# A mixture-of-experts stage that sends each token only to its two chosen experts

## The chip, the cores and the metric

The kernel runs on one core of one Trainium2 chip. The metric is the device time of one execution, in microseconds (us). The trace comes from one profiled execution on the same kind of core; its engines are TensorE (PE, with the loading of weights shown apart as PEld), VectorE (DVE), ScalarE (ACT), GpSimd (POOL) and SyncE (SP), which only issues transfers here.

## What is computed

Two layers over 2048 tokens (4 batches of 512) of width 128. Each layer adds `s * silu(ffn)` to `x`, where `s` comes from an attention and `ffn` from a mixture of experts on the normalised `x`. The change is in the second layer's mixture:

```python
def _L1_ffn_ref(x, wg1, bg1, wg2, w_in, w_out):
    # E, H, K, G = 8, 256, 2, 32
    xt = x.reshape(-1, d)
    g = gelu(xt @ wg1 + bg1)
    probs = softmax(g @ wg2)
    top_vals, top_idx = top_k(probs, K)
    gates = zeros_like(probs).at[arange(n)[:, None], top_idx].set(top_vals)
    h = gelu(einsum('nd,edh->enh', xt, w_in))
    o = einsum('enh,ehd->end', h, w_out)
    y = einsum('ne,end->nd', gates, o)
```

Only two of the eight rows of `gates` are not zero for a token. The result of this mixture is used late, as the gate of the second layer's output: `x + s * silu(y)`.

## The kernel before

The work falls into four stages on one time line. First comes the first layer's mixture (`norm_ffn0`, 0 to 78 us in the trace) with the loading of the weights. Then the first layer's attention (`attn0`, 78 to 400 us) goes through 32 segments of 64 positions. Then the second layer's mixture (`ffn1`, 392 to 534 us). Last is the second layer's attention (`attn1`, 534 us to the end), 16 steps for each of the 4 batches.

Nearly every instruction is pinned: `pin`, `mm1`, `act1`, `vec1`, `pool1` and `dma1` (L314 to L330) record an operation and keep it in program order on its engine. So each engine works through a list written by hand, and an instruction that waits holds up all that stands behind it on its engine. The DMA queue of SP is such a list too, and so are the transfers that POOL issues. The lists are made by dictionaries of the form "after step n, also call these functions" (`between` in `attn0` and `ffn1`), and in `attn1` by the number t of the step.

In one segment n of `attn0`, TensorE makes the scores of the next segment, then `memory(n)` (L709, tiles `mm`), `update(n)` (L726, tiles `mu`), `attend(n)` (L753, tiles `dot`) and `attended(n-1)` (L776, transposes `pa`). POOL multiplies by gates and adds: L724 in `memory`, L740 in `update` (a part of the memory `mz`, which TensorE reads in `memory(n+1)`), L772 and L773 in `attend`, whose result the transposes `pa` read. The router of the second layer's first two batches is already run inside `attn0` (`sums`, `scale`, `normed`, `turned`, `hidden`, `logits`, `chosen` at segments 18 to 24).

The second layer's mixture before is dense: `ffn1` (L979) goes over 4 batches and 8 experts, 32 units in all. A unit is `up(b, e)` (L946: two matmuls 128x512 in fp32, which the trace shows as four, into tile `ph`; then one gelu on ACT) and, one unit later, `down(b, e)` (L956: eight matmuls 128x128 into tile `eo`, 16 in the trace; then four DVE operations L969 or L971 that weight the result with `gw` and add it to `acc`). Between units stand the end of `attn0` (`left[0]`, `left[1]`), the router of batches 2 and 3, and the preparation of the second attention for batch 0 (`prepare1`), whose tiles are `ptk`, `ptv`, `ptq`, `pjk`, `pjq` and `pl`, and whose DRAM pieces `kd`, `qd`, `qe` are written by SP. `opening1` (L1552) at the last unit makes the first scores of the second attention from operands that SP loads (`k<-kd`, `q<-qd`).

In a step i of `attn1` (b = i // 16, t = i % 16), TensorE makes the scores of step i+1 (`s`), then three groups of products with the values (`acc`); ACT makes `exp` and squares; DVE multiplies the two (L1548, tiles `e`), and the third group of the next step's products needs that. Side work is spread over t. At t = 11, `gate1` (L994) turns the mixture's result into the gate. POOL prepares the features of the next batch and the products L1324 and L1325 of rows that SP has loaded.

At the end a flag says whether the fast path's bounds held; if not, `run_any` computes all again on a general path.

Of the kernel before, what the change touches and what calls it, by code (L numbers as in the profile page):

```python
# [11 lines left out]

# [28 lines left out]
HF, G1 = 256, 32  # L41

# [52 lines left out]
class Kernel:  # L95
# [124 lines left out]
    def load_second(self, pool):  # L220
# [3 lines left out]
        for w in ("q", "k", "v"):  # L224
            own = pool.tile([P, D], F32, name=f"l1w{w}")
            nc.sync.dma_start(out=own, in_=i[f"L1_attn_W{w}"])

            flat = pool.tile([P, D], F32, name=f"l1b{w}f")
            nc.gpsimd.dma_start(out=flat, in_=i[f"L1_attn_b{w}"].partition_broadcast(P))
            self.wt[w] = pool.tile([P, D], F32, name=f"l1w{w}t")  # L230
            self.bt[w] = pool.tile([P, D], F32, name=f"l1b{w}t")
            for to, src in ((self.wt[w], own), (self.bt[w], flat)):
                nc.gpsimd.tensor_copy(
                    to.rearrange("p (m r d) -> p m r d", m=4, r=4),
                    src.rearrange("p (r m d) -> p m r d", m=4, r=4),
                )
            if w != "v":
                self.b1[w] = pool.tile([P, 1], F32, name=f"l1b{w}")
                own = i[f"L1_attn_b{w}"].rearrange("(r m d o) -> m r d o", m=4, r=4, o=1)
                for m in range(4):  # L240
                    nc.gpsimd.dma_start(out=self.b1[w][m * 32 : m * 32 + 32], in_=own[m])
# [63 lines left out]
    def normed(self, pool, mv, rstd, layer, n):  # L305
        xn = pool.tile([P, D], F32, name=f"xn{layer}_{n}", tag="xn", bufs=4)
        self.vec1(self.nc.vector.tensor_scalar(
            xn, self.x[:, n, :], mv[:, n, 0:1], rstd[:, n : n + 1], ALU.subtract, ALU.mult
        ))
        return xn  # L310
# [561 lines left out]

    def begin_ffn1(self, pool, psum, layer):
# [7 lines left out]
        gw = pool.tile([P, NT, NE], F32, name=f"gw{layer}")  # L881
        xnT, acc, xn, hid, out = {}, {}, {}, {}, {}
# [44 lines left out]
        def chosen(b):  # L927
# [11 lines left out]
            at = pool.tile([P, 4, 2, NE], F32, name=name("at", b), tag="at", bufs=2)  # L939
            self.vec1(v.tensor_tensor(  # L940
                at, bc(bc(self.iota, 1, 2), 1, 4), bc(idf, 3, NE), ALU.is_equal
            ))
            self.vec1(v.tensor_mul(at, at, bc(top[:, tiles(b), 0:2], 3, NE)))
            self.vec1(v.tensor_add(gw[:, tiles(b), :], at[:, :, 0], at[:, :, 1]))

# [10 lines left out]
        def down(b, e):  # L956
# [19 lines left out]
            sums, scale, normed, turned, hidden, logits, chosen, up, down  # L976
        )}, xnT=xnT, acc=acc)

    def ffn1(self, first, between, begun=False):  # L979


        late = None
        for b in range(B):
            for e in range(NE):
                if not (begun and late is None):
                    first.up(b, e)
                for f, *args in between.get((b, e), []):
                    f(*args)
                if late:
                    first.down(*late)  # L990
                late = b, e
        first.down(*late)
# [63 lines left out]
    def mixing1(self, pool, keep, psum):  # L1056
# [6 lines left out]
        self.load_second(keep)  # L1063
# [84 lines left out]
    def begin1(self):  # L1148

        nc, keep = self.nc, self.keep1  # L1150
        self.bounds = keep.tile([P, 2 * B * H1 + 2], F32, name="bounds")

        self.feat = keep.tile([P, 16, ROWS1 + P], F32, name="feat")
        nc.gpsimd.memset(self.feat[:, :, ROWS1 - 1 : ROWS1], 1.0)
        self.sets1 = []
        for k in range(2):
            strip = keep.tile([P, 4, H1, STRIP], F32, name=f"strip{k}")
            nc.gpsimd.memset(strip, 0.0)
            nc.gpsimd.memset(strip[:, :, :, 26:27], 1.0)
            lin = keep.tile([P, 2, 4, 4, 32], F32, name=f"lin{k}")  # L1160
            nc.gpsimd.memset(lin, 0.0)
            self.sets1.append((strip, lin))

        self.rows1 = keep.tile([P, 4, S], F32, name="rows1")
        self.rows2 = keep.tile([P, 4, S], F32, name="rows2")
        self.now1, self.banks1, self.inv1, self.prod1 = {}, {}, {}, {}

# [255 lines left out]
    def large1(self, flag):  # L1423
# [3 lines left out]
        every = pool.tile([P, nb + 2], F32, name="every")  # L1427

        def first():
# [3 lines left out]
            ))  # L1433
            self.pool1(nc.gpsimd.partition_all_reduce(every, bounds, P, bass_isa.ReduceOp.max))

        def second():
# [5 lines left out]
            bad = pool.tile([P, 3], F32, name="bad")  # L1442
            for k, (value, limit) in enumerate((
                (most, (LIMIT / SCALE1) ** 2), (every[:, nb : nb + 1], SUM_MAX),
                (every[:, nb + 1 : nb + 2], -SUM_MIN),
# [113 lines left out]
    def attn1(self, xnT, g1):  # L1559
# [4 lines left out]
        with tc.tile_pool(name="a1", bufs=2) as self.a1, tc.tile_pool(  # L1564
# [59 lines left out]
            for i in range(n):  # L1624
                b, t = i // 16, i % 16
                if t == 11:
# [32 lines left out]
                if b == B - 1 and t in (3, 11):  # L1659
                    large[t // 8]()  # L1660
                late = [f for f in [rest(x) for rest, x in ready] if f]
# [302 lines left out]
    def run(self):  # L1964
# [15 lines left out]
        with tc.tile_pool(name="wf1", bufs=1) as wf1, tc.tile_pool(name="f1", bufs=1) as f1:  # L1980
            stack = ExitStack()
            w0 = stack.enter_context(tc.tile_pool(name="w0", bufs=1))
            with tc.tile_pool(name="wf0", bufs=1) as wf0:
                self.load_first(wf0, w0)
                xnT, g0 = self.norm_ffn0(0, lambda pool, psum: self.mixing1(pool, late, psum))
                self.load_memory(w0)
            self.load_experts(wf1)
            with tc.tile_pool(name="ap", bufs=1, space=PSUM) as psum:
# [8 lines left out]
                    24: [(first.chosen, 1)], 30.5: [(first.up, 0, 0)],  # L1997
                })
                second, prep = ExitStack(), []

                def begin():
                    stack.close()
                    keep, a1q, dram = (
                        tc.tile_pool(name="a1k", bufs=1, side="right"),
                        tc.tile_pool(name="a1q", bufs=1, side="right"),
                        tc.tile_pool(name="a1d", bufs=2, space=bass.MemoryType.DRAM),
                    )
                    self.keep1, self.a1q, self.a1d = map(second.enter_context, (keep, a1q, dram))
                    self.begin1()
                    prep.extend(self.prepare1(0, first.xnT, psum, ("t", 2)).values())  # L2010

                def prepare():
                    pe, rest, *evict = prep.pop(0)
                    ps = pe()
                    rest(evict[0](ps) if evict else ps)

                between = {
                    (0, 1): [(left[0],)], (0, 2): [(left[1],), (begin,)], (0, 3): [(first.sums, 2)],
                    (0, 4): [(first.sums, 3)], (0, 5): [(first.scale, 2, 4), (first.normed, 2)],
                    (0, 6): [(first.turned, 2), (first.normed, 3)],  # L2020
                    (0, 7): [(first.turned, 3), (first.hidden, 2)],
                    (1, 0): [(first.hidden, 3)], (1, 1): [(first.logits, 2), (first.logits, 3)],
                    (1, 2): [(first.chosen, 2)], (1, 4): [(first.chosen, 3)],
                }
                for k in range(11):
                    between[1 + (5 + k) // NE, (5 + k) % NE] = [(prepare,)]
                between[B - 1, NE - 1] = [(self.opening1, psum, "w", 3)]
                self.ffn1(first, between, True)
# [6 lines left out]
    def run_any(self):  # L2035

        tc = self.tc
        with tc.tile_pool(name="wf1c", bufs=1) as wf1:
# [6 lines left out]
            with tc.tile_pool(name="f1c", bufs=1) as pool, tc.tile_pool(  # L2045
# [6 lines left out]
                for b in range(B):  # L2052
                    for f in ("normed", "turned", "hidden", "logits", "chosen"):
                        getattr(first, f)(b)
                self.ffn1(first, {})
# [40 lines left out]
```

## Time and profile before

| | us |
|---|---|
| median of 3 timed runs (lowest, highest) | 888.13 (888.01, 890.93) |
| the profiled execution | 890.56 |
| its span in the trace | 888.8 |
| stage of the second layer's mixture, 400 to 534 us: PE busy of 134.0 | 131.7 |
| the same stage: DVE, ACT, POOL busy | 53.2, 44.8, 24.6 |
| second attention, 534 to 585 us: PE, DVE, ACT, POOL busy of 51.0 | 48.4, 38.9, 43.0, 40.9 |
| second attention, 622 us to the end: PE, DVE, ACT, POOL busy of 267 | 248.3, 193.9, 183.7, 108.9 |

A row of the timeline has the start in us, the length in us, the engine, the line of the kernel, the operation, `output<-input`, the shapes, and how many such instructions were merged. In brackets stands how long the engine was idle just before, and whose end it waited for. A group row ends with busy time, mean length of one in ns, and the idle time before.

### The profile page before, as it was taken

To read this page: it belongs to the slowest core of one execution; us is meant where nothing else is said; L and a number is where in the kernel's file an instruction comes from. 1 tells how busy PE (TensorE), PEld (TensorE's weight loads), DVE (VectorE), ACT (ScalarE), POOL (GpSimd) and SP (SyncE) were. 2 spreads that over 40 slices of the span, in tenths; PEclk is the share of its full clock that TensorE was granted. 3 is DMA by queue.
4 is the path that set the end of the run, shared out by engine and by line. 5 is a ranking of instruction groups with operands and counts; after the bars stand their busy time and mean duration, and the time that the engine had idled before them with its cause. 6 is when DMAs were issued, how large, how long until landed. Compare 5 with 4: busy or idle time off the path is not lost. (4 is left out here: it accounts for less than half of the span.)

```text
span 888.8 us, 19127 instructions
## 1 busy us (share of the span) xinstructions
PE 850.0 (96%) x7660; PEld 525.9 (59%) x7660; DVE 596.3 (67%) x1202; ACT 520.1 (59%) x692; POOL 383.4 (43%) x471
## 2 busy tenths in 40 slices
PE   8998899999999999989999998999999999989996
PEld 4565688898888969877677772333234224322324
DVE  7774666667668868863353337687876888677684
ACT  3433565656566665642432249778776787768780
POOL 7840244545444433563033007853934492441112
PEclk9999999999999989999999999999999999999999
DMA  8501421212122121100005002354151324130000
GB/s 213 140 14 39 117 62 43 80 25 84 37 61 72 38 60 37 27 1 1 1 1 178 1 1 72 126 164 110 53 172 53 87 92 128 58 87 30 1 13 15
DMA packets 77055, 57.64 MB, mean 65 GB/s; under 512 B 40176, under 2 KB 65040, under 8 KB 76960
## 3 DMA queue, kind: packets, MB, share of 16 engines
q1 hardware_dynamic: 74768, 54.94, 21.1%
q0 software_dynamic: 1616, 1.16, 0.8%
q8 instruction: 62, 1.02, 0.5%
q10 hardware_dynamic: 576, 0.26, 0.1%
q14 instruction: 33, 0.27, 0.1%
HBM read 35.36 MB, written 20.97 MB: 63 GB/s over the span
## 5 line engine op out<-in xcount | busy, mean ns | idle before, releaser
L1548 DVE TENSOR_TENSOR e<-e,e 128x1024 f32<-128x1024 f32 x126 | 182.2, 1486 | 78.1 <-ACT e L321 78.1
L318 PE MATMUL acc<-e,strip 128*32 128x512 f32 x1520 | 185.0, 601 | 11.8 <-DVE bank L1590 10.4
L321 ACT ACTIVATE e<-s 128x1024 f32<-128x1024 f32 x126 | 122.1, 1022 | 69.0 <-PE s L318 69.0
L321 ACT ACTIVATE e<-e 128x1024 f32<-128x1024 f32 x126 | 126.4, 1060 | 0.0
L318 PEld LDWEIGHTS acc<-e,strip 128*32 128x32 f32 x1520 | 44.9, 110 | 125.5 <-issue 86.6
L321 ACT ACTIVATE h<-ph 128x1024 f32<-128x1024 f32 x32 | 32.8, 1024 | 87.5 <-PE ph L318 87.4
L318 PEld LDWEIGHTS eo<-w_out,h 128*128 128x128 f32 x512 | 62.5, 196 | 11.7 <-issue 10.4
L321 ACT ACTIVATE pj<-pp 128x512 f32<-128x512 f32 x64 | 38.2, 597 | 50.4 <-PE pp L318 50.2
L318 PE MATMUL eo<-w_out,h 128*128 128x128 f32 x512 | 64.5, 281 | 1.0 <-DVE g L971 0.8
L772 POOL TENSOR_TENSOR t<-t,gate 128x512 f32<-128x512 f32 x32 | 40.8, 1276 | 56.9 <-DVE t L705 41.7
L971 DVE SCALAR_TENSOR_TENSOR g<-eo,gw,g 128x128 f32<-128x128 f32 x112 | 31.5, 344 | 48.7 <-PE eo L318 48.7
L318 PE MATMUL dot<-vone,E 128*128 128x65 f32 x512 | 61.1, 273 | 0.0
L318 PEld LDWEIGHTS dot<-vone,E 128*128 128x128 f32 x512 | 59.8, 192 | 1.1 <-issue 0.8
L318 PE MATMUL ph<-xnT,w_in 128*128 128x512 f32 x128 | 60.3, 594 | 0.0
L724 POOL TENSOR_TENSOR t<-t,gate 128x512 f32<-128x512 f32 x32 | 40.9, 1279 | 33.7 <-DVE t L705 33.7
L747 DVE TENSOR_TENSOR mz<-mz,mu 64x512 f32<-64x512 f32 x56 | 38.4, 685 | 19.3 <-PE mu L318 18.7
L667 DVE SCALAR_TENSOR_TENSOR elu<-elu,up 128x512 f32<-128x512 f32 x60 | 42.4, 707 | 7.2 <-ACT up L321 6.4
L773 POOL TENSOR_TENSOR t<-t,t 128x512 f32<-128x512 f32 x32 | 45.7, 1429 | 2.5
L321 ACT ACTIVATE attT<-pa 128x512 f32<-128x512 f32 x32 | 19.1, 597 | 46.2 <-PE pa L783 46.2
L643 DVE TENSOR_TENSOR E<-sc,cap 128x1024 f32<-128x1024 f32 x32 | 39.0, 1220 | 9.6 <-PE sc L318 7.0
L740 POOL TENSOR_TENSOR mz<-mz,zs 64x8 f32<-64x8 f32 x56 | 11.7, 209 | 70.3 <-DVE zs L672 61.6
L321 ACT ACTIVATE E<-E 128x1024 f32<-128x1024 f32 x32 | 33.6, 1051 | 11.5 <-DVE E L643 11.5
(279 smaller groups left out, 1629.4 us busy)
## 6 DMA issues: line engine op xcount, KB each, us to landing
vd<-vt SPq DMA_DIRECT2D x32, 256.0 KB
vone<-vd SPq DMA_DIRECT2D x64, 128.0 KB
k<-kd SPq DMA_DIRECT2D x16, 256.0 KB
q<-qd SPq DMA_DIRECT2D x16, 256.0 KB
rows<-qd SPq DMA_DIRECT2D x64, 64.0 KB
other<-qe SPq DMA_DIRECT2D x16, 256.0 KB
kd<-partk SPq DMA_DIRECT2D x12, 256.0 KB
qd<-partq SPq DMA_DIRECT2D x12, 256.0 KB
```

The lines of the kernel that those rows point to most:

```text
L318: return self.pin(self.nc.tensor.matmul(*args, **kw))
L321: return self.pin(self.nc.scalar.activation(*args, **kw))
L643: self.vec1(nc.vector.tensor_tensor(e.rearrange("p x hp c -> p (x hp) c"), ps.rearrange("p x hp c -> p (x hp) c"), bc(self.cap.rearrange(" ...
L667: self.vec1(nc.vector.scalar_tensor_tensor(t, t, 1.0, up, ALU.min, ALU.add))
L724: nc.gpsimd.tensor_mul(t, t, self.gate)
L740: nc.gpsimd.tensor_add(new[half, :, :, p, DK].rearrange("d hp a -> d (hp a)"), old[half, :, :, p, DK].rearrange("d hp a -> d (hp a)"), seg ...
L747: self.vec1(nc.vector.tensor_tensor(new[half, :, :, p, 0:DK], old[half, :, :, p, 0:DK], ps[half, :, :, p * 64 : p * 64 + 64].rearrange("d ...
L772: nc.gpsimd.tensor_mul(t, t, gate2)
L773: nc.gpsimd.tensor_add(t, t, seg[n]["t1"])
L971: self.vec1(v.scalar_tensor_tensor(acc[b][:, k, :], eo[:, k, :], w, acc[b][:, k, :], ALU.mult, ALU.add))
L1548: self.vec1(self.nc.vector.tensor_mul(t, src[0][pair], src[1][pair]))
```

## The change

The second layer's mixture no longer runs every expert on every token. The tokens are taken in two halves of two batches (1024 tokens, 2048 choices each). For each half, 8 experts have 512 places each in a DRAM tensor (`rows_in`), which is filled with zeros at the start of the program. The choice of a token gets a place: its rank among the choices of that expert so far, from matmuls with a triangular and an all-ones matrix (`placed`). POOL then writes each token's normalised row to its two places by indirect DMAs (`sent`: 8 for a batch, 128 rows of 512 bytes each). A unit is now one expert of one half: SP fetches 512 rows (`fetched`), TensorE turns them (`faced`), `up1`, `gelu1` and `down1` follow, and SP writes the result to `rows_out`. That makes 16 units in place of 32. In `attn1` POOL gathers, for each batch, the two result rows of each token by 8 indirect DMAs at t = 8 (`back1`), and DVE weights and adds them at t = 10 (`together`); the gate follows at t = 12 in place of 11. If an expert of a half gets more than 512 tokens, the flag sends the program to the general path, which keeps the dense form.

With that, things move. The place and the sending of batches 0 and 1 stand at segments 24 to 26 of `attn0`; the fetches of the first two units at segment 29; the end of `attn0` now comes before unit 1 without expert work between; the router of batches 2 and 3 stands at units 0 to 4; and `prepare1` runs in another order, from unit 0 on. Half of the clearing of the second attention's tiles (`zeros1(1)`) moves to step 0 of `attn1`.

```diff
+    def begin_rows(self, pool, dram):
+        spill = (NE + 1) * ROOM
+        self.rows_in = [dram.tile([spill + 16 * P, D], F32, name=f"in{h}") for h in range(2)]
+        self.rows_out = [dram.tile([NE * ROOM, D], F32, name=f"out{h}") for h in range(2)]
+        zero = pool.tile([P, S], F32, name="zero")
+        nc.gpsimd.memset(zero, 0.0)
+        for t in self.rows_in:
+            nc.sync.dma_start(
+                out=t[0 : NE * ROOM].rearrange("(p n r) d -> p n (r d)", p=P, r=4),
+                in_=bc(zero, 1, NE),
+            )
...
+        def placed(b):
+            (at, e), own = hid[b], mask[:, tiles(b)]
+            self.vec1(v.tensor_copy(self.share[:, tiles(b)], top[:, tiles(b), 0:2]))
+            self.vec1(v.tensor_add(own, at[:, :, 0], at[:, :, 1]))
+            ps = narrow("rank", b)[:, :, 0:NE]
+            parts = [(ps, self.lower, own)]
+            parts += [(ps[:, k + 1 :], self.ones, bc(own[:, k], 1, 3 - k)) for k in range(3)]
+            if b % 2:
+                parts += [(ps, self.ones, bc(mask[:, b * 4 - 4 + k], 1, 4)) for k in range(4)]
+            for k, (out_, lhsT, rhs) in enumerate(parts):
+                self.mm1(
+                    out_, lhsT=lhsT, rhs=rhs, start=(k == 0), stop=(k == len(parts) - 1)
+                )
+            self.vec1(v.tensor_tensor(at, at, bc(ps, 2, 2), ALU.mult))
...
+        def sent(b):
+            for k in range(4):
+                for c in range(2):
+                    self.pool1(nc.gpsimd.indirect_dma_start(
+                        out=self.places[b // 2][b % 2 * 8 + k * 2 + c],
+                        out_offset=bass.IndirectOffsetOnAxis(
+                            ap=self.slots[:, b * 4 + k, c : c + 1], axis=0
+                        ),
+                        in_=xn[b][k], in_offset=None,
+                    ))
...
+        def faced(i):
+            pt = narrow("xgt", i)
+            for k in range(4):
+                self.pin(nc.tensor.transpose(pt[:, k, :], out["in", i][:, k], self.ident))
+            out["t", i] = pool.tile([P, 4, P], F32, name=name("xt", i), tag="xt", bufs=2)
+            self.act1(out["t", i], pt, AF.Copy)
...
+    def ffn1(self, first, between):
+        n = 2 * NE
+        for i in range(n):
+            if i:
+                first.up1(i)
+            first.gelu1(i)
+            for f, *args in between.get(i, []):
+                f(*args)
+            if i + 1 < n:
+                first.faced(i + 1)
+            for k in [i + 3] if i + 3 < NE else [NE, NE + 1] if i == NE - 2 else [i + 3] * (
+                NE - 2 < i < n - 3
+            ):
+                first.fetched(k)
+            if i:
+                first.down1(i - 1)
+        first.down1(n - 1)
+
+    def back1(self, b):
+        nc, acc = self.nc, self.of_batch("g", 1, b)
+        other = self.a1.tile([P, 4, D], F32, name=f"bk{b}", tag="pr1", bufs=2)
+        for c, t in enumerate((acc, other)):
+            for k in range(4):
+                self.pool1(nc.gpsimd.indirect_dma_start(
+                    out=t[:, k, :], out_offset=None, in_=self.rows_out[b // 2][:],
+                    in_offset=bass.IndirectOffsetOnAxis(
+                        ap=self.found[:, b * 4 + k, c : c + 1], axis=0
+                    ),
+                ))
...
+                if i == 0:
+                    self.zeros1(1)
+                if t == 8:
+                    g1[b], together = self.back1(b)
+                if t == 12:
                     self.gate1(pool, g1[b], b)
...
+                if t == 10:
+                    together()
...
-                    24: [(first.chosen, 1)], 30.5: [(first.up, 0, 0)],
+                    24: [(first.chosen, 1), (first.placed, 0)],
+                    25: [(first.placed, 1), (first.sent, 0)], 26: [(first.sent, 1)],
+                    29: [(first.fetched, 0), (first.fetched, 1)], 30.5: [(first.faced, 0)],
                 })
+                left[0]()
+                first.up1(0)
+                first.fetched(2)
+                left[1]()
...
+                        0: [(prepare, 2), (first.sums, 2), (first.sums, 3), (first.scale, 2, 4)],
+                        1: [(prepare, 3), (first.normed, 2), (first.turned, 2)],
+                        2: [(first.normed, 3), (first.turned, 3), (first.hidden, 2)],
+                        3: [(first.hidden, 3), (first.logits, 2), (first.logits, 3),
+                            (first.chosen, 2), (first.chosen, 3)],
+                        4: [(first.placed, 2), (first.sent, 2), (first.placed, 3),
+                            (first.sent, 3)],
+                        5: [(prepare, 0)], 7: [(prepare, 1), (prepare, 9)],
+                        10: [(prepare, 4)], 11: [(prepare, 5)], 12: [(prepare, 6), (prepare, 7)],
+                        13: [(prepare, 8)], 14: [(prepare, 10)],
+                        15: [(self.opening1, psum, "w", 3)],
```

`up1`, `gelu1` and `down1` have the matmuls of `up` and `down`, and `down1` ends with one DVE copy of the whole tile `eo` and a transfer to `rows_out`.

## Prediction

> **What bounds the kernel now.** I read the page's timeline first, then the group rows, then TensorE's order of time in the stage that the change rewrites.
>
> ```profile
> span 888.8 us, 19127 instructions
> ...
> PE   8998899999999999989999998999999999989996
> ...
> POOL 7840244545444433563033007853934492441112
> ...
> L318 PE MATMUL eo<-w_out,h 128*128 128x128 f32 x512 | 64.5, 281 | 1.0 <-DVE g L971 0.8
> ...
> L318 PE MATMUL ph<-xnT,w_in 128*128 128x512 f32 x128 | 60.3, 594 | 0.0
> ```
>
> TensorE is busy nearly everywhere, and `ph` and `eo` of the second mixture waited for next to nothing. So that stage is TensorE's. A unit's cadence, from TensorE's order of time:
>
> ```profile
> 411.17 1.88 PE L318 MATMUL ph<-xnT,w_in 128*128 128x512 f32 x4
> 412.89 1.95 PE L318 MATMUL eo<-w_out,h 128*128 128x128 f32 x16
> 414.68 1.88 PE L318 MATMUL ph<-xnT,w_in 128*128 128x512 f32 x4
> ```
>
> From start to start `ph` takes 1.72 us and `eo` 1.79, so 3.51 for a unit, 112 for all 32. The change halves that. What it adds is mostly on POOL, and waits.
>
> **The unknown price, c.** The trace has no indirect DMA. Let c be the time for which one holds POOL; there are 32 writes and 32 gathers. Nearest rows of POOL's order of time, and landing from the table of issues:
>
> ```profile
> 3.06 0.54 POOL L116 DMA_DIRECT2D sg<-in_L_ffn_Sg_dram  x1
> ...
> 810.02 1.50 POOL L1434 PARTITION_ALL_REDUCE every<-bounds  x1 [7.13 <-DVE bounds L1431]
> ```
> ```profile
> sg<-in_L_ffn_Sg_dram POOLq DMA_DIRECT2D x1, 64.0 KB, 2.9
> ```
>
> `sg` moves the same 128 rows of 512 bytes without indices: 0.54, the lower end; indices can't make it cheaper. The only instruction in which POOL works across partitions takes 1.50, the upper end. I take 0.75: the direct issue plus 0.21, POOL's mean for its smallest two-input operation (`mz<-mz,zs`, 64x8), for reading the 128 indices. It is nearest to the direct row because the work differs by the indices only. Landing: 2.5 us after issue (rows of 64 KB: 2.5 to 3.5). [...]
>
> **Part by part** (c = 0.75 in brackets).
>
> *Start.* POOL gets five small operations ahead of `pick0b`, about 1.3 us, against 2.3 us between the end of `pick0b` (13.84) and the first `pw` (16.18). SP gets 4 MB of zeros behind the first weights; DVE's first use of a late load is at 47.95, with inputs ready at 42. 0 to 3, I take 0.5.
>
> *Router places in `attn0`.* `rank` of batch 0 stands behind `pa` at 341.0. It needs DVE's mask, which is queued behind `chosen` of batch 1:
>
> ```profile
> 345.31 0.23 DVE L940 TENSOR_TENSOR at<-iota,idf 128x64 f32<-128x64 f32 x1
> ```
>
> With two small operations that is 345.9: TensorE, without idle time from 341 to 362, waits 5.0, and the matmuls are 0.4. Batch 1's `rank` waits from 353.3 to 354.8 for the mask behind DVE's `t`, plus 0.6. Together +7.5.
>
> *Sending from `attn0`.* The first eight writes stand behind POOL's 357.5, ahead of these:
>
> ```profile
> 357.88 1.28 POOL L724 TENSOR_TENSOR t<-t,gate 128x512 f32<-128x512 f32 x1 [0.36 <-DVE t L705]
> 361.26 0.49 POOL L740 TENSOR_TENSOR mz<-mz,zs 64x8 f32<-64x8 f32 x2 [2.09 <-DVE zs L672]
> ```
> ```profile
> 363.17 1.11 PE L318 MATMUL mm<-mz,elu 128*64 128x130 f32 x16
> ```
>
> `mm` reads `mz`. With the writes `mz` ends at 357.5 + 8c + 1.77, so `mm` loses 8c − 3.9. After L772 and L773 (2.9) come the next eight; `mz` then ends at 364 + 16c, against `mm` of the next segment at 369.2 + (8c − 3.9): again 8c − 1.3. Sum 16c − 5.2 (6.8). The segments after it have no idle time to give it back.
>
> *End of `attn0`.* 1.75 of `ph` leaves, 0.55 of turning comes: `pa` of segment 31, which waits for POOL, comes 1.2 earlier. −1.2.
>
> *The mixture.* Before, from that `pa` (399.79) to the second score tile (534.06): 134.3. After, TensorE's work: 16 `ph` 27.5; 16 `eo` 28.6; 15 turnings of four transposes at 0.53 (from `lnt`) 8.0; `pa` 0.5; `po` 3.8; router (two `lnt`, two `pgr`, two `lp`) 4.9; `rank` 1.2; preparation `pjk`, `pjq` 1.9, `ptk`, `ptv`, `ptq` 2.7, four `pl` 6.0; scores 0.5. Sum 85.6. Its waits: the copy of the second turned tile stands on ACT behind the router's square root, whose sums need the last `po`: 0.4 `sg`, 0.8 POOL's add, 3.2 statistics, 1.6 table load and root, 0.6 copy, less TensorE's own work: 5.1. Small ACT waits at units 2 to 4: 0.5. `rank` of batches 2 and 3 behind two `chosen` of 2.6 and two exponentials: 5.3. The first scores: SP now loads `k` and `q` behind the result of unit 13, so copy 0.8, three issues 1.5, landing 5 less `ph` 1.7: 5.5. The change of pools 1.3, as before. Together 103.3: −31.0.
>
> Then a term f. Unit 8 can't be fetched before all 16 writes of batches 2 and 3 have landed. They start 1.1 before the last `rank` ends, and TensorE has 15.5 of work from there to unit 8's turning. So f = 16c + 2.5 + 0.2 + fetch − 16.6. A fetch of 256 KB I take at 5.0, between 2.9 (the 64 KB row) and 7.3 (`other<-qe` in the chain). f = 16c − 8.9 (3.1).
>
> *`attn1`.* In batch 0 POOL is busy until the products end, and the gathers stand behind them; `together` stands ahead of the `e` at 585.96:
>
> ```profile
> 582.44 2.17 POOL L1325 TENSOR_TENSOR rows<-rows,other 128x512 f32<-128x512 f32 x1
> ```
> ```profile
> 585.96 2.36 DVE L1548 TENSOR_TENSOR e<-e,e 128x1024 f32<-128x1024 f32 x2 [0.27 <-ACT e L321]
> ```
>
> They land at 584.6 + 8c + 2.5. DVE stands from 585.7, then needs 2.4 (eight operations at 0.30); everything of DVE queues behind, `e` first, which TensorE wants 4.5 us later than it came. 8c − 0.8 (5.2). In the other batches POOL was idle for 13.5 us from there (657.1 to 670.7), and DVE had 1.3 and 2.7 idle beside `y`: 1 in all; 5 more where c passes 1.3. [...]
>
> Sum: 0.5 + 7.5 + 6.8 − 1.2 − 31.0 + 3.1 + 5.2 + 1 = −8.1; in general 40c − 38.1. From the profiled execution's 890.56 (span 888.8 and 1.8 around it) that gives 882.5. That execution lay 2.4 above the median of 888.13, so as a median I say 880.
>
> **Rivals.** (1) *POOL becomes the bound* and the kernel gets slower. Place: sending at segments 25 and 26, unit 8's fetch, gathers of batch 0. It decides from c = 0.95, where the sum is zero; at c = 1.3 it is +18.9 with the other batches' 5, so 907. For: 40 of every us of c reach the end, and POOL stands in the path at three places. Against: the direct issue is only 0.54. (2) *Indices cost nothing*: c = 0.54, f = 0, sum −16.3, so 872; 864 if 8 of the 18 us of router waits are hidden. For: direct issues lie between 0.50 and 0.63 whatever their shape. (3) *About the same*, c between 0.85 and 1.05: −4 to +4. (4) *The change doesn't do what it says*: over 512 tokens for one expert, and the general path runs. The reference's own routing gives at most 411. 1 in 100.
>
> **Chances.** A measurement can tell about 0.5% (4.4 us) from no change. My forecast, c from 0.65 to 0.85: 0.30. (2): 0.20. (3): 0.14. (1): 0.35. (4): 0.01. So faster 0.50, same 0.14, slower 0.36. The sign is close to open, and the range takes in both: 864 from (2), 908 from (1); beyond c = 1.3 it leaves out about 1 in 10. The forecast's own range is 874 to 884.
>
> **What would show it.** The indirect rows on POOL give c at once. `mm` waiting for POOL `mz` in two segments after 360 shows the sending; `xgt` of unit 8 waiting for its DMA shows f; DVE waiting for gathers at t = 10 of batch 0 shows the last. `ph` must count 64 and `eo` of this stage 256. I am wrong if TensorE's waits for `rank` are absent, if the mixture's fetches lag in every unit, or if zeros hold up the start.

## The result and the profile after

| us | before | after |
|---|---|---|
| median (lowest, highest) | 888.07 (885.84, 890.93) | 921.57 (915.94, 929.33) |
| profiled execution, its span | 890.56, 888.8 | 915.94, 914.1 |
| start to the last `pa` of the first attention | 399.8 | 422.0 (+22.2) |
| from there to the second score tile `s` (mixture) | 134.3 | 116.9 (−17.4) |
| from there to the end (second attention) | 354.8 | 375.3 (+20.5) |
| TensorE's clock at half, all pieces added | 16.4 | 76.6 |

The ratio is 1.038, 95% interval 1.030 to 1.047: slower by 3.8%, where 0.9% faster was forecast. The page of the kernel after, its span, slices and two groups:

```profile
span 914.1 us, 18790 instructions
...
PE   8998899999999979697968979969999999989896
...
POOL 7660254454544433755454207973766586551512
PEclk9999999999999998878988999979999999999998
...
L1024 POOL DMA_INDIRECT in<-xn,slots x32 | 31.8, 995 | 27.0 <-DVE slots L1017 17.9
...
L322 PE MATMUL eo<-w_out,h 128*128 128x128 f32 x256 | 35.1, 295 | 10.1 <-DVE y L1071 8.6
```

`eo` halved as planned. But PE has holes from the fifteenth slice on, and the granted clock falls to 7 in two slices. In the page before it is nowhere under 8:

```profile
PEclk9999999999999989999999999999999999999999
```

The order of time on POOL gives c:

```profile
366.12 0.96 POOL L1024 DMA_INDIRECT in<-xn,slots x1 [0.30 <-issue]
367.39 0.96 POOL L1024 DMA_INDIRECT in<-xn,slots x1 [0.30 <-issue]
368.65 0.96 POOL L1024 DMA_INDIRECT in<-xn,slots x1 [0.30 <-issue]
```

From start to start an indirect DMA holds POOL for 1.27: 0.96 and a pause of 0.30. The waits between 355 and 400 us, while 16 of them run, show something the prediction had no term for:

```profile
ACT pj L325 <- remote: 6.4, 1, 6.4
...
ACT attT L325 <- remote: 5.2, 1, 5.2
...
PE pa L787 <- ACT pj L325: 4.8, 1, 4.8
```
```profile
385.41 0.53 PE L322 MATMUL mm<-mz,elu 128*64 128x130 f32 x5 [0.28 <-issue]
386.86 0.34 PE L322 MATMUL mm<-mz,elu 128*64 128x130 f32 x2 [0.92 <-issue]
388.30 0.45 PE L322 MATMUL mm<-mz,elu 128*64 128x130 f32 x3 [1.09 <-issue]
```

"Remote" means that nothing on this core's engines explains the end of the wait, "issue" that the engine waited for nothing visible. ACT's `pj` needs only matmuls that ended, by their records, at 365.87. The trace also holds the times at which semaphores change; through them one engine signals to another that an instruction has ended. In the kernel before, each engine's signal comes within 0.3 of the instruction that gives it (14 to 25 ns for a matmul). Here TensorE's signal for those matmuls comes at 373.59, 7.7 late and 1.5 after the last of eight writes, and three more within 0.25 of it. In the mixture the latest comes 11.1 late: the `ph` that ended at 474.55, for which ACT waits.

```profile
472.66 1.88 PE L322 MATMUL ph<-xt,w_in 128*128 128x512 f32 x4
485.68 1.02 ACT L325 ACTIVATE h<-ph 128x1024 f32<-128x1024 f32 x1 [13.55 <-remote]
```

The late signals are TensorE's. Of DVE's, ACT's and POOL's signals all that the trace holds up to 913 us lie within 0.04 of the end of an instruction. Some records of signals are missing beside runs of indirect DMAs (16 of DVE's 913, 14 of ACT's 656, 9 of TensorE's 794 here, none before), so the next record after an end is not always that instruction's own. And the ends of matmuls are modelled in the trace, so a late signal can't be told from a matmul that ended late.

So two theories were set against each other. **P**: only the time for which POOL is held counts, and my sum is right once c is. **S**: indirect DMAs also hold back the other engines' signals (TensorE's, by the records), and the waits that follow halve TensorE's clock.

### The profile page after: what moved, and what is told of

Same layout as the page of the kernel before. It is cut to its first block, busy times and chain, and to the rows that moved or that the text cites. A ratio compares the mean times of both kernels' runs of the same rounds, so it can differ in the third digit from the quotient of the medians.

```text
span 914.1 us, 18790 instructions
## 1 busy us (share of the span) xinstructions
PE 829.5 (91%) x7428; PEld 505.9 (55%) x7428; DVE 594.6 (65%) x1152; ACT 512.8 (56%) x692; POOL 461.6 (50%) x540
## 4 chain that ended last, share of the span: by engine, by line
PE 64%; DVE 13%; issue 7%; DMA 6%; POOL 4%; ACT 4%; SPq 1%; another core or an unknown queue 1%; DVEq 0%; POOLq 0%; ACTq 0%
PE acc L322 9%; PE pp L322 6%; PE dot L322 6%; PE eo L322 5%; DVE e L1720 5%; PE po L322 5%; PE sc L322 4%; PE mm L322 3%; PE mu L322 3%; PE ph L322 3%; PE pv L322 2%; ACT e L325 2%; DMA other<-qe 2%; PE s L322 2%; PE pk L683 2%
## 5 line engine op out<-in xcount | busy, mean ns | idle before, releaser
L1720 DVE TENSOR_TENSOR e<-e,e 128x1024 f32<-128x1024 f32 x126 | 189.8, 1546 | 68.2 <-ACT e L325 68.1
L322 PE MATMUL acc<-e,strip 128*32 128x512 f32 x1520 | 189.1, 601 | 23.9 <-DVE e L1720 12.2
L322 PE MATMUL dot<-vone,E 128*128 128x65 f32 x512 | 63.2, 277 | 0.6 <-issue 0.5
L728 POOL TENSOR_TENSOR t<-t,gate 128x512 f32<-128x512 f32 x32 | 40.9, 1279 | 33.5 <-DVE t L709 33.4
L751 DVE TENSOR_TENSOR mz<-mz,mu 64x512 f32<-64x512 f32 x56 | 38.4, 685 | 22.8 <-PE mu L322 17.4
L1071 DVE COPY y<-eo 128x512 f32<-128x512 f32 x16 | 11.1, 691 | 55.5 <-PE eo L322 41.1
L325 ACT ACTIVATE h<-ph 128x1024 f32<-128x1024 f32 x16 | 16.4, 1024 | 53.5 <-PE ph L322 35.6
L777 POOL TENSOR_TENSOR t<-t,t 128x512 f32<-128x512 f32 x32 | 45.1, 1408 | 2.5
L1024 POOL DMA_INDIRECT in<-xn,slots x32 | 31.8, 995 | 27.0 <-DVE slots L1017 17.9
L322 PE MATMUL eo<-w_out,h 128*128 128x128 f32 x256 | 35.1, 295 | 10.1 <-DVE y L1071 8.6
L322 PE MATMUL s<-q,k 32*128 32x512 bf16 x512 | 39.9, 387 | 3.8 <-DMA q<-qd 3.0
L1568 POOL TENSOR_TENSOR pr<-pr,pr 128x512 f32<-128x512 f32 x14 | 21.5, 1552 | 41.7 <-DVE pr L1563 41.7
```

Source lines behind the costliest of these rows:

```text
L322: return self.pin(self.nc.tensor.matmul(*args, **kw))
L325: return self.pin(self.nc.scalar.activation(*args, **kw))
L728: nc.gpsimd.tensor_mul(t, t, self.gate)
L751: self.vec1(nc.vector.tensor_tensor(new[half, :, :, p, 0:DK], old[half, :, :, p, 0:DK], ps[half, :, :, p * 64 : p * 64 + 64].rearrange("d ...
L777: nc.gpsimd.tensor_add(t, t, seg[n]["t1"])
L1024: self.pool1(nc.gpsimd.indirect_dma_start(out=self.places[b // 2][b % 2 * 8 + k * 2 + c], out_offset=bass.IndirectOffsetOnAxis(ap=self.slo ...
```

## Experiments

**1. Direct DMAs, with POOL held less, nearly as long, and a little longer.**

```diff
-self.pool1(nc.gpsimd.indirect_dma_start(out=self.places[b // 2][r], ..., in_=xn[b][k], ...))
+self.pool1(nc.gpsimd.dma_start(out=self.places[b // 2][r][r * P : (r + 1) * P], in_=xn[b][k]))
+self.pool1(nc.gpsimd.memset(self.blank, 0.0))               # second and third kernel
+self.pool1(nc.gpsimd.memset(self.blank[:, 0:256], 0.0))     # third kernel
```

> All 32 writes and 32 gathers become direct DMAs of POOL, of the same 128 rows of 512 bytes, to and from fixed places; a small POOL copy that reads the places stands ahead of each eight writes, so that they still wait for them. It leaves out the routing: experts get the wrong rows. Theory P (only the time for which POOL is held counts; the sum of the prediction is right if c is put right): c falls from 1.27 to 0.54 to 0.65, so 40c - 38.1 gives 871 to 878. Theory S (indirect DMAs also hold back the signals by which other engines release each other, and the waits that come of it halve TensorE's clock): the same time as P says or a little above it, but the waits in which ACT, DVE and TensorE stand with nothing of the profile to release them (6.4 and 5.2 of ACT, 12.1 of DVE ahead of y) are gone. Theory Q (any run of DMAs from POOL holds back the signals): those waits stay, and the time is over 900.

> As the kernel with direct DMAs, but each of the 64 is followed by a POOL memset of 128x512 (0.59 in the trace) into a tile that nobody reads, so that POOL is held for about 1.2 for each, nearly the 1.27 of an indirect one. The routing is left out. Theory P: c of 1.2 gives -38.1 + 48 + 4 for the other batches, +14, so 902, and the time stays within 1 percent of the changed kernel's 916 to 922. Theory S: POOL's hold is only part of it: the signals are prompt, TensorE's half-speed time falls from about 70 us to under 45, and the time is 895 to 903. Theory Q: over 915.

> The changed kernel with direct DMAs, each followed by POOL memsets of 128x512 and 128x256, so that POOL is held for about 1.27 for each, as by an indirect one (with the memset of 128x512 alone it was about 1.0, and the time 898.7). The routing is left out. What remains up to the changed kernel's 921.6 is then due to the indirect DMAs themselves. Theory P: 915 to 922. Theory S: 903 to 911, with no late signal; the sum of the prediction at c = 1.27 says 905.

Measured: 882.57 (ratio 0.9905, 0.9869 to 0.9940) with c = 0.53, above the 871 to 878 that were expected; 898.67 (1.0116, 1.0076 to 1.0156) with c about 1.0; 906.37 (1.0209, 1.0174 to 1.0245) with c = 1.39. The third was meant to hold POOL as long as the indirect DMAs do, 1.27, but holds it a little longer, from start to start:

```profile
364.74 0.54 POOL L1032 DMA_DIRECT2D in<-xn  x1
366.13 0.54 POOL L1032 DMA_DIRECT2D in<-xn  x1
```

No signal in any of the three is over 0.3 late, and no wait is put down to "remote"; so theory Q is out. POOL's hold alone, from 0.53 to 1.39, makes 24. Although the indirect DMAs hold POOL for less, the kernel after is 15.2 slower in the medians (10.2 in the profiled executions). Interpolated between the second and the third kernel, a hold of 1.27 gives some 904, an estimate. So both theories have a part. By stages, against before: first attention +17.9 with direct DMAs at 1.39 and +22.2 after; mixture −16.0 and −17.4; second attention +13.3 and +20.5.

One thing more differs in the first attention. POOL's four operations of a segment at L728 to L777 aren't pinned. After, they stand behind all eight writes of a batch; in the third kernel they slip in between, here after four:

```profile
367.14 1.28 POOL L728 TENSOR_TENSOR t<-t,gate 128x512 f32<-128x512 f32 x1
```

So the 4.3 between the two kernels there isn't shown to be the late signals' alone.

The mixture loses about the same either way, by different waits. Waits from 455 to 500 us with direct DMAs at 1.39:

```profile
DVE tokq L1374 <- POOL feat L1395: 12.3, 1, 12.3
...
PE xgt L1051 <- DVE tokq L1374: 7.8, 1, 7.8
```

and from 460 to 490 us after:

```profile
ACT h L325 <- remote: 13.5, 1, 13.5
...
PE eo L322 <- DVE y L1071: 8.6, 1, 8.6
```

With prompt signals DVE stands before `tokq`, because POOL's products of the first tokens (`feat`) are queued behind the 16 writes; with late signals TensorE waits about as long for `y`. They lie beside each other: prompt signals alone, with POOL held so long, brought nothing here.

**2. Unused DMAs in quiet segments of the kernel before.**

```diff
+for k in range(8):
+    self.pool1(nc.gpsimd.indirect_dma_start(out=views[j][k],
+        out_offset=bass.IndirectOffsetOnAxis(ap=at[:, k : k + 1], axis=0), in_=self.ident, ...))
```

> The kernel before, with DMAs added that nobody uses, in quiet segments of the first attention: 8 indirect writes behind segment 2, 8 direct writes behind 6, 8 indirect gathers behind 10, and 8 indirect writes, two a segment, behind 13 to 16. All move 128 rows of 512 bytes. Nothing is left out. Theory P: POOL is held for 10 us by each eight indirect ones and 4.5 by the direct ones, and TensorE waits for POOL's part of the memory by about 6, 0, 6 and 0. Theory S: behind segments 2 and 10 ACT, DVE and TensorE stand for several us with nothing of the profile to release them, as in the changed kernel, with none of that behind 6, and with little behind 13 to 16. Theory Q: also behind 6.

> The kernel before, with unused DMAs in quiet segments of the first attention: 4 indirect writes of 128 rows in a row behind segment 2; 8 behind segment 6 with a POOL memset of 128x512 (0.6) after each; 3 in a row behind segment 10; 8 of 16 rows each behind segment 14. Nothing is left out. If signals are held back for as long as a run lasts, 4 in a row delay by up to 3 and cost 0 to 2; the 8 with memsets delay by under 1.5 at a time, as every gap lets signals through, though POOL is held for 15 us and TensorE waits for POOL by some 5 to 9; 3 in a row cost 0. If the number of rows matters and not the instruction, 8 of 16 rows delay nothing.

What each run delayed the later segments by, and how late TensorE's latest signal was, each record being put to the instruction that makes the lateness least:

| run | cost | TensorE's latest signal |
|---|---|---|
| 8 indirect writes | 6.84 | 5.8 |
| 8 indirect gathers | 3.83 | 5.8 |
| 8 direct writes | 0.00 | under 0.3 |
| 8 indirect writes in pairs, a pair to a segment | 0.00 | 1.25 |
| 4 indirect writes | 0.00 | 1.0 |
| 3 indirect writes | 0.00 | under 0.3 |
| 8 indirect writes, a memset after each | 8.5 | 0.5 |
| 8 indirect writes of 16 rows | 7.5 | 6.8 |

Groups of POOL in the two probes (128 rows written, gathered and written directly; then 16 rows):

```profile
L2005 POOL DMA_INDIRECT to<-ident,at x16 | 15.8, 985 | 4.2 <-issue 3.9 <-DMA to<-ident,at 0.3
L2019 POOL DMA_INDIRECT got<-to,at x8 | 7.7, 961 | 2.3 <-issue 2.0 <-DMA got<-to,at 0.3
L2013 POOL DMA_DIRECT2D to<-ident x8 | 4.4, 555 | 0.0
```
```profile
L2032 POOL DMA_INDIRECT to<-ident,at x8 | 6.8, 845 | 2.3 <-issue 2.0 <-DMA to<-ident,at 0.3
```

The hold belongs to the instruction, not to its rows: 112 rows less save only 0.14, and signals are late beside 16 rows too. In a run of eight they fall behind by several us; with a memset after each they are nearly prompt, but a gap made of POOL's own work costs POOL's time instead. Three or four in a row, or pairs, cost nothing here: the segments had that much slack.

**3. The clock.** Five unused matmuls fill the wait for the first ranks.

```diff
+whole = narrow("rank", b)
+for _ in range(5 if b == 0 else 0):
+    self.mm1(whole, lhsT=self.ident, rhs=xnT[0], start=True, stop=True)
```

> The changed kernel with five matmuls of 128x512 whose result is not used, put on TensorE ahead of the ranks of batch 0, where it waits 4.75 for VectorE's mask. Nothing is left out. If the wait halves TensorE's clock afterwards, then with the wait filled the half-speed stretch of 6.8 after 341 is gone, the scores and the output behind it take 1.16 and 3.74 rather than 2.08 and 5.11, and segment 24 ends 2 to 2.5 earlier. If the clock has nothing to do with the wait, segment 24 ends no earlier or up to 0.5 later.

TensorE's order of time after, then in this kernel:

```profile
343.19 0.21 PE L322 MATMUL rank<-mask,lower 128*128 128x32 bf16 x1 [4.75 <-DVE mask L997]
...
343.38 2.08 PE L322 MATMUL sc<-pj,pj 64*128 64x128 f32 x16
345.25 5.11 PE L322 MATMUL po<-l0wo,attT 64*128 64x128 f32 x64
```
```profile
343.11 0.18 PE L322 MATMUL rank<-mask,lower 128*128 128x32 bf16 x1 [0.46 <-DVE mask L997]
...
343.28 1.16 PE L322 MATMUL sc<-pj,pj 64*128 64x128 f32 x16
344.28 3.74 PE L322 MATMUL po<-l0wo,attT 64*128 64x128 f32 x64
```

The half-speed stretch of 6.8 that began at 341.3 is gone, and segment 24 ends 2.35 earlier, though the ranks come no sooner. So the wait of 4.75 cost 7.1, half as much again. For the granted clock the traces before and after hold two values only, 1.0 and 0.5; the pieces at 0.5 last 3.41, 6.83, 10.24 or 17.07, apart from the last, 2.70 before and 4.91 after. How a wait brings the clock to 0.5 is not shown.

**4. The second attention.** Two edits, apart: batch 0's gathers in pairs, and the clearing of tiles, moved into the mixture; and the last results in tiles of their own.

```diff
+9: [(prepare, 6), (self.zeros1, 1)], 10: [(prepare, 4), (first.paced, 10), (self.early1, 0)], ...
```
```diff
+y = self.top.tile([P, 4, D], F32, name=name("y", i), tag=f"g{i - 12}")     # for units 13 to 15
```

> The changed kernel with two things of the second attention moved into the mixture: the clearing of the second set of tiles to unit 9, and batch 0's eight gathers to units 10 to 13, two a unit (each pair behind a small POOL copy that waits for that unit's gelu), with their weighting at unit 14. Nothing is left out. Theory S: the 20.5 that the second attention lost sit in these two places alone (about 5 at its first steps, 15 at steps 12 and 13), so it falls to 0 to 3, and the pairs cost the mixture 0 to 4; the time is 901 to 907. Theory P gives the gathers alone 9.4 of the 20.5, so 907 to 912. Rival: eight gathers hold back signals wherever they stand, and the mixture loses as much as the attention wins: 917 to 922.

> The changed kernel, with one edit: the results of the last three units are copied into tiles that outlive the mixture, so that the second attention's first tiles, which take over the mixture's memory, no longer wait for the last write of a result to land. Nothing is left out. If that wait (ACT 6.7 and VectorE 4.7 on the write of y) is the cause of the 3.6 to 5.3 at the first steps of the second attention, in the kernels with direct DMAs too, they fall to under 1 and the second attention from 375.3 to 370 to 372. If it is the moved clearing of tiles, nothing changes there.

The first: 906.17 (1.0171, 1.0110 to 1.0231); the second attention costs +7.5 in place of +20.5, with nothing left at steps 12 and 13, where 15.5 had been lost. The mixture went up by 2.6. Of the 7.5, 3.6 still stand at the first steps, so the clearing was not their cause. The second kernel (916.2 in a single run) shows what was; ACT after, and with the tiles apart:

```profile
543.64 1.94 ACT L325 ACTIVATE e<-s 128x1024 f32<-128x1024 f32 x2 [5.47 <-DMA out<-y]
```
```profile
543.23 1.94 ACT L325 ACTIVATE e<-s 128x1024 f32<-128x1024 f32 x2 [2.93 <-PE s L322]
```

The attention's first tiles take over the mixture's memory, and so wait until the last `y` has been written to DRAM. Without that the first five steps lose 0.0, and the second attention 17.1. In batches 1 to 3 the same eight gathers cost nothing in any kernel (from step 21 to step 48 the loss changes by at most 0.7).

**5. The first attention.** Spread writes, late and early:

```diff
+25: [(first.placed, 0), (first.sent, 0, 0, 2)], 26: [(first.placed, 1), (first.sent, 0, 2, 4)], ...
```
```diff
+10: [(first.sums, 0)], 11: [(first.scale, 0, 1), (first.normed, 0)], ... 16: [(first.placed, 0)],
+17: [(first.sent, 0, 0, 2)], ... 24: [(first.placed, 1), (first.sent, 1, 0, 2)], ...
```

> The changed kernel, but in the first attention the places of batches 0 and 1 are made one segment later (behind 25 and 26), the 16 writes are spread in twos and threes over segments 25 to 30, and the first two fetches and turnings come only at the end of that attention. Nothing is left out. Theory P: POOL carries the same work, the two TensorE waits for ranks (4.8 and 1.2) go, and the first fetch is waited for by about 6 to 8: the time stays within 4 us of the changed kernel's. Theory S: runs of two or three don't hold back signals for long, so the 12 us of such waits in segments 25 to 27 shrink to under 4 and less of the stage is at half clock; end of the first attention 8 to 14 earlier, less 6 to 8 for the fetch.

> The changed kernel with the first attention alone edited: batch 0's router runs at segments 10 to 16 rather than 18 to 24, its writes in pairs at 17 to 20; batch 1's places are made at 24, a segment behind its choice, and its writes stand in pairs at 24 to 27. Nothing is left out. The second square root and gelu cost ACT more changes of table. Theory S: as the pairs in quiet segments cost nothing, the end of the first attention falls from 422 to 400 to 407, and the time to 900 to 907. Theory P: the pairs of batch 0 cost nothing, those of batch 1 in the short segments 26 and 27 some 3, the rank waits are gone (6): 404 to 408, and nearly the same time; so this run tells what the cure is worth, and the rows in which signals are late tell the theories apart (none over 2 us).

Late: 911.43 (1.0268, 1.0207 to 1.0329). Early: 909.9 (1.0225, 1.0169 to 1.0280), with the end at 412.4, and not at the 400 to 408 that I expected: with the router in two parts segment 23 ends 7.0 later than before, where after it had ended 2.6 earlier. ACT's second changes of tables may be in that (one `ACT_TABLE_LOAD` takes 1.28 in the traces before and after); it wasn't taken apart. TensorE's signals are at most 1.1 late there.

**6. All together.**

> As the run with all cures, but the mixture's router and its 16 writes stay as in the changed kernel. Nothing is left out. First attention to 408 to 413, mixture 117 to 120 with the pairs of gathers in it, second attention 355 to 358: 884 to 893. If the gains don't add up, because a stage that begins earlier only waits longer for the same transfer, over 897.

> The run with all cures but the mixture's, with every indirect DMA made direct, as in the first direct run; the routing is left out. It is the bound for what cheaper indices could give: no late signals, c of 0.54 to 0.65. First attention to 403 to 409, mixture 108, second attention 355 to 357: 868 to 876, and 12 to 18 under the same kernel with indirect ones. Theory P alone would have the two differ by 5 or less, as the pairs and the moved gathers lie beside other work.

> The kernel with all cures but the mixture's, in which only the 16 writes of the mixture are direct; those of the first attention and all gathers stay indirect. The routing of batches 2 and 3 is left out. If late signals and POOL's longer hold in the mixture are the whole of what that stage still loses, it falls from 119 to 105 to 108, the first and second attention stay at 410 and 355, and the time is 872 to 878. If the early gathers or the half-speed clock after other waits carry it, the stage stays over 112.

> All cures at once: batch 0's router, and the writes of batches 0 and 1 in pairs, in the earlier segments; the clearing and the gathers of batch 0 in the mixture; the last results in tiles of their own; and in the mixture batch 2's router begins at segment 26 of the first attention, the 16 writes of batches 2 and 3 stand in groups of two or three at units 2 to 7, each behind a wait for that unit's gelu, and the preparation of the second attention follows later. Nothing is left out. Theory S: the wait of 8.6 in the mixture shrinks to under 3 and the stage from 117 to 108 to 113; with 401 to 410 at the end of the first attention and 355 to 358 for the second the time is 872 to 888. Rival: three indirect DMAs to a unit are as bad as a run of 16, as POOL has no gap; the mixture stays at 115 or more, and the time is 885 to 895.

Without the last edit, the mixture's, the cures add up: 888.66 (1.0006, 0.9974 to 1.0039), as fast as before. With all DMAs direct 872.69 (0.9826, 0.9788 to 0.9863), with only the mixture's writes direct 880.85 (0.9856, 0.9799 to 0.9912), where 872 to 878 were expected. In these two the mixture takes 105.2 and 105.3, against 119.0: there the price of indices sits. Spreading its writes by two or three a unit, with an earlier router, failed: 895.79 (1.0062, 1.0028 to 1.0097), the first attention 12 longer and the mixture still 118.2. No late signal is to be seen in its mixture; TensorE waits for the fetch of unit 8, my term f, behind the spread writes:

```profile
480.14 1.09 PE L1051 MATMUL xgt<-ident,xg 128*128 128x128 f32 x4 [9.21 <-DMA xg<-in]
```

In that kernel the fetches of units 8 and 9 also stand in the list ahead of the last two writes, so it leaves out the last two writes' rows for these units.

**7. The mixture again.** Groups of four writes with memsets between them, and the tokens and forms of the preparation ahead; then a common router a segment earlier; then two waits moved.

```diff
+if b > 1 and (k * 2 + c) % 4 == 3:
+    for _ in range(2):
+        self.pool1(nc.gpsimd.memset(self.blank, 0.0))
```
```diff
+if i == 0:
+    first.faced(1)          # ahead of the router's square root
...
+12: [..., (self.operands1, 0, 0), (self.operands1, 0, 1)],
```

> As the kernel with all cures but the mixture's, and in the mixture the 16 writes in groups of four with two POOL memsets of 128x512 (1.1) after each group, and the preparation's tokens and forms moved from units 5 to 13 to units 2 to 7, so that TensorE has 6 us more of its own work before unit 8. Nothing is left out. Theory S: groups of four held back signals by up to 3.1 in the quiet segments and cost nothing there, so the wait of 8 goes; the fetch of unit 8 comes 4 later, covered by the forms; mixture 107 to 113, time 876 to 884. If gaps of 1.1 aren't enough, the wait stays over 5 and the stage at 115 or more.

> As the kernel with groups in the mixture, and in the first attention the routers of batches 0 and 1 together again, a segment earlier than in the changed kernel (18 to 23), places a segment behind the choice (23 and 24), and the 16 writes in groups of two or three over segments 23 to 28, the first fetches at 30. Nothing is left out. One change of table for both instead of two: 2 to 5 earlier at segment 23; groups of three in the long segments cost nothing, POOL's hold in segments 26 to 28 costs 2 to 5. End of the first attention 405 to 410 against 410, time 873 to 884. If POOL's hold in the short segments outweighs it, 412 to 418.

> The kernel with groups and the compact router, with two more waits of the mixture moved: the turning of unit 1 and its copy stand ahead of the router's square root on ACT (TensorE waited 3.6 for that copy), and the operands of the second attention's first scores are loaded at unit 12 rather than behind the last results (it waited 4.5 for them). Nothing is left out. If these waits are on the path, the mixture falls from 115.7 to 106 to 111 and the time from 887 to 877 to 883, under both kernels; if the late signals take their place, the stage stays over 113 and the time at 885 or more.

888.29 (0.9995, 0.9966 to 1.0024), 887.08 (0.9980, 0.9954 to 1.0005) and 884.58 (0.9949, 0.9925 to 0.9974). The last is faster than both kernels, by 0.5% than before and 4% than after, with everything computed; but the first two lie above the ranges expected of them, and the third just above its own. Its mixture takes 111.7. There, with the products ahead and none of TensorE's signals over 0.3 late, TensorE waits for what my term f named, the fetch of unit 8 (2.4 and 3.4 in the first two kernels of this part); the waits from 413 to 525 us, and the page's clock, which is at half for 48 us in all:

```profile
PE xgt L1055 <- DMA xg<-in: 6.8, 2, 6.4
```
```profile
span 883.5 us, 18802 instructions
...
PEclk9999999999999999996989999999999999999999
```

## Why the prediction was wrong

| term | predicted, c = 0.75 | the same at c = 1.27 | direct, held 1.39 | after |
|---|---|---|---|---|
| to the end of the first attention (16c + 1.6) | 13.6 | 21.9 | 17.9 | 22.2 |
| mixture (16c − 39.9) | −27.9 | −19.6 | −16.0 | −17.4 |
| second attention (8c + 0.2) | 6.2 | 10.4 | 13.3 | 20.5 |
| sum (40c − 38.1) | −8.1 | 12.7 | 15.2 | 25.3 |

- *"I take 0.75 ... because the work differs by the indices only."* This step failed, and it decided the sign. The real c is 1.27, within my bounds, near the upper end, which I had set aside. Of the 1.27 the instruction itself takes 0.96, against 0.54 for a direct one, and 112 more indices cost only 0.14 in the probes. At 1.27 my sum gives +12.7, rival 1. At 1.39 it gives +17.5, and direct DMAs held so long gave +15.2. So POOL becoming the bound was the right mechanism, from the right point, and I gave it 0.35.
- *Late signals* were no term and no rival. What the indirect DMAs add beyond POOL's hold, at least the step from 15.2 to 25.3 (15 by the medians), stands mostly in the second attention (7.2) and the first (4.3). That late signals are the whole of it is argued, not shown: in the first attention POOL's order differs too, and in the second the gathers also landed later.
- *Router places in `attn0`, +7.5.* The waits came as computed (4.75 and 1.23 against 5.0 and 1.5). The first cost 2.35 more through the clock. Ahead of them stands a gain of 2.6 at segment 23 that I hadn't counted.
- *Sending, 16c − 5.2.* 15.1 at the real c; 17.2 measured by segment 28. With direct DMAs at 1.39 it is 12.9 against 17.0 by the formula, where POOL's products slip in between the writes.
- *The mixture, f = 16c − 8.9.* 11.4 at the real c; 8.6 was lost there, but not at the place I gave: unit 8 didn't wait for its fetch in the kernel after. Beside the writes stood late signals, or with prompt ones POOL's `feat`; the wait for the fetch came once the writes were spread or the work around them was moved (2.4 to 9.2). I had queued the writes against SP alone and hadn't asked what POOL does next.
- *"The change of pools 1.3, as before."* That pool now holds tiles that a DMA reads; the loss at the first steps of the second attention is 1.6 to 5.5 in the kernels that keep it, 5.3 after.
- *Batch 0's gathers, 8c − 0.8.* With direct ones 3.9 (step 12 to 13) against 3.4 by the formula at 0.53; held for 1.39, 10.2 against 10.3; after, 15.5 against 9.4. The landing, which I put at 2.5, took 5.3 after and 4.8 with direct DMAs at 1.39 (2.4 to 3.2 in the other batches). The waits between 588 and 612 us after:

```profile
PE acc L322 <- DVE e L1720: 8.8, 2, 8.6
ACT e L325 <- remote: 8.5, 1, 8.5
```

and DVE's order after, then with direct DMAs at 1.39:

```profile
606.99 0.35 DVE L1146 SCALAR_TENSOR_TENSOR g<-bk,share,g 128x128 f32<-128x128 f32 x1 [0.67 <-DMA bk<-out,found]
607.26 4.26 DVE L1720 TENSOR_TENSOR e<-e,e 128x1024 f32<-128x1024 f32 x2
```
```profile
603.06 0.46 DVE L1152 SCALAR_TENSOR_TENSOR g<-bk,share,g 128x128 f32<-128x128 f32 x1 [0.81 <-DMA bk<-out]
603.44 2.76 DVE L1726 TENSOR_TENSOR e<-e,e 128x1024 f32<-128x1024 f32 x2
```

The order is as I gave it: TensorE waits for `e`, which stands behind the last gather. After, ACT got its scores 5.6 late (the `remote` wait), so the two `e` take 1.5 longer, and TensorE's half clock behind the wait lasts 17.1 against 6.8. How the rest divides between landing, late scores and clock wasn't taken apart.

- *Other batches, 1*: nothing, as forecast; the eight gathers took 11.5 to 12.3 there.

## What to carry to other kernels

Price an indirect DMA by the instruction, not by its rows (0.99 us for 128 rows and 0.85 for 16 in the probes, without the pause of 0.30), ask what its engine would have done next, and what the tiles that take over the memory wait for. A wait of TensorE can also cost clock afterwards: here one of 4.75 cost 2.35 more, half its length again. Put indirect DMAs where their engine is idle and where nobody waits for TensorE soon; in quiet segments pairs and threes cost nothing here (0.00), but in the short segments writes in twos and threes left a wait of TensorE of 6.41 for POOL's `t` ahead of the last `pa`, and in the mixture they left the stage at 118.2.

## What was not expected of the hardware

Beside a run of indirect DMAs TensorE's signals come late, by up to 11.1 us in the mixture after, and mostly nearly at once when the run ends (some came during it, 2.0 and 3.2 late); beside direct DMAs from the same queue they don't (under 0.3), and beside pairs in quiet segments hardly (1.25). It is shown that the engines which need these signals stand until they come: ACT starts `h` at 485.68, after 13.55 idle, just behind the signal at 485.66. By what way is open, also whether the signal is late or the matmul itself, and whether the recording of the profile, which loses records at these places, has a part.

What else decides is open too. The same eight gathers make signals up to 6.0 late in batch 0 after, and 1.1 at most in the other three. The same groups of four in the mixture made them 1.2 late in two kernels of part 7 and not at all in the third, in which none is late anywhere, though its first attention is the same as the second's, where they are up to 2.9 late. That third profile was taken on another chip, so execution or chip may decide. The medians of kernels with indirect DMAs stand on wider spreads (915.9 to 929.3 after) than those with direct ones (905.8 to 910.7 at 1.39). None of this was tried.

A caution on reading stages: two single traces of the same code can differ. The first attention ended at 422.0 after and at 426.6 with the early gathers, which stand far behind it; a difference of a few us in one stage of one trace is shown only where the traces agree ahead of it, as the traces after and with direct DMAs at 1.39 do, to 0.1 up to segment 22.
